# Moving the kernel products of heads 16 to 31 and three of the last eight evacuations in a long-convolution and gated-FFN kernel

## The chip, the cores and the metric

The kernel runs on one core of a Trainium2 chip. The metric is the device time of one execution in microseconds (us), the median of several runs. One execution was also taken by the hardware profiler; its times are those of the profile below.

## The reference

Two parts follow each other. The first is a state-space convolution: each of 64 heads has a kernel of 1024 taps, a sum over 64 complex exponentials, and every sequence (32 of them, masked to its length) is convolved with it. The second is a gated FFN with 4-bit weights, whose result is added to the input.

```python
K = 2.0 * einsum('hn,hnl->hl', Cs, exp(dtA[:, :, None] * arange(L))).real   # 64 heads, 1024 taps
y = irfft(rfft(u_m, n=2 * L) * rfft(K, n=2 * L))[..., :L] + u_m * D[:, None]
y = y * mask
gate, up = y2 @ Wg, y2 @ Wu              # 1024 -> 2752, 4-bit weights, one scale per 128 inputs
out = (gate * sigmoid(gate) * up) @ Wd   # 2752 -> 1024
x = x + out
```

## The kernel before

The kernel K of a head is a product of two small factors, since exp((32a + b) dtA) = exp(32a dtA) exp(b dtA). `tables` and `factors` make the factors on ScalarE (sine, square) and VectorE (lines 189 to 220; `e1t` by L220 is the last of them). `make_kernel` (L397) then forms the product for eight heads on TensorE (L401 for the D term, L403 for the factors, all in f32), ScalarE copies it as f16 (L406), VectorE subtracts the copy for the low f16 half (L407), and two DMAs on SP's queue write both halves to a padded array in DRAM, `kpad` (L409). `toeplitz` (L488, its DMA L499) loads from it, with overlapping rows, a head's Toeplitz matrix of 128 x 2 x 1024 f16 (512 KB).

`conv_head` (L505) convolves one head: 24 matmuls (L521) in 8 steps, and after every second head VectorE multiplies the PSUM result by the mask into `y` (L533), ScalarE rounds it to the f16 tile `xh` (L536), and GpSimd, for the last pair VectorE, makes the low half `xl` (L538). `conv(0)` is heads 0 to 15, `conv(1)` heads 16 to 31. Its PSUM tiles `cq` come from the pool "a", two single banks; the pool "b" holds three pairs of banks. 16 heads are one block of 512 columns of the FFN's input.

The FFN runs as chains. A chain (`gu_one` for one block, `gu_pair` for two, `dn_pair` for the down projection) runs over groups of 128 inputs: four matmuls of 512 columns, then a rescale in place in PSUM by the ratio of two groups' scales, on VectorE or ScalarE, whichever a running estimate, `lag`, has less work for (L584, L587, L604, L608). `gu_one`'s matmuls are L618 (on `xh`) and L619 (on `xl`), `gu_pair`'s L639 and L640, `dn_pair`'s L677, L678 and, for the last group, L680. Up to four chains are under way. `roll` (L706) writes their order by hand, in rounds of one step for each active chain, and advances side generators at set rates: in stage 0, beside the four `gu_one` chains of block 0, `second()` at five steps for each chain step.

The first convolution, ahead of stage 0, is a loop over its 128 steps (L853). At set step numbers it issues other work: step 7 the product of heads 8 to 15, the factors of heads 16 to 31 and two input splits (`kernel_8`), step 40 the product of heads 16 to 23, step 56 the scale ratios, step 72 the product of heads 24 to 31, step 100 the load of the inputs of heads 16 to 19. Every eighth step from 32 to 104 advances the unpacking of the 4-bit weights (loads L552 and L553, VectorE L556 and L566, GpSimd L562). `second()` (L860) then makes the ratios of the down projection, issues the Toeplitz loads of heads 16 to 21, closes the pool `kg`, lets six steps pass and runs `conv(1)`. A scheduler puts the instructions on the engines by priority, so that an instruction can stand somewhat earlier or later in its engine's queue than its place in the source; each engine then works in order.

At the end, `dn_pair` of block 3 adds to the input: ScalarE scales each half of a chain's result into `o` (L693), VectorE adds it to the residual (L694; in the earlier blocks GpSimd does), and SP stores 256 KB (L695).

Of the kernel before, what the change touches and what calls it, by code (L numbers as in the profile page):

```python
# [16 lines left out]
AF = mybir.ActivationFunctionType  # L17
ALU = mybir.AluOpType
# [237 lines left out]
class Core:  # L256
# [410 lines left out]
    def dn_pair(self, k, blk, place):  # L667
        nc = self.nc
        self.need(*(("dn", k, half) for half in range(2)))
        q = self.psum("chq", place)  # L670
        for g in range(GI):
            while blk % 2 == 1 and g < 21 and not self.loaded.get((blk, g)):
                yield
            for j in range(2):
                lw = self.wd[k][:, g, 128 * j:128 * j + 128]
                if g < 21:
                    nc.tensor.matmul(q[:, j], lw, self.ihl[:, g, 0], start=(g == 0), stop=False, skip_group_check=True)  # L677
                    nc.tensor.matmul(q[:, j], lw, self.ihl[:, g, 1], start=False, stop=False, skip_group_check=True)  # L678
                else:
                    nc.tensor.matmul(q[:, j], lw, self.ic[blk % 2], start=False, stop=True, skip_group_check=True)  # L680
            if g < 21:
                self.rescale_two(q, self.rdn[:, 2 * k:2 * k + 2, g:g + 1])
                self.passed[blk, g] = self.passed.get((blk, g), 0) + 1
                if blk % 2 == 0 and self.passed[blk, g] == 4:
                    nc.sync.dma_start(self.ihl[:, g], self.spill[g])
                    self.loaded[blk + 1, g] = True
                yield
        xr = self.res[k] if blk == 3 else self.residual(self.fw, 2 * k, blk)
        o = self.fw.tile([128, 2, 512], F16, name="o", bufs=2)
        self.act(1180)  # L690
        for j in range(2):
            n = 2 * k + j
            nc.scalar.activation(o[:, j], q[:, j], AF.Copy, scale=self.ldn[:, n:n + 1])  # L693
            (nc.gpsimd if blk < 3 else nc.vector).tensor_tensor(xr[:, j], xr[:, j], o[:, j], ALU.add)  # L694
            nc.sync.dma_start(self.io["out"][128 * n:128 * n + 128, 512 * blk:512 * blk + 512], xr[:, j])  # L695
        yield

# [70 lines left out]
def tile_ssm_ffn(ctx, tc, io):  # L768
    nc = tc.nc
    c = Core(ctx, tc, io)  # L770
# [14 lines left out]
    kg = kg_stack.enter_context(tc.tile_pool(name="kg", bufs=1))  # L785
# [49 lines left out]
    def ratios_dn():  # L835
        c.rdn, c.ldn = c.scale_ratios(c.sdn, GH, GI, "dn", [(0, 8, 0, 128, 16.0)])
# [11 lines left out]
    def load_16():  # L848
        c.us[4] = c.conv_load(16)

    events = {7: kernel_8, 40: lambda: c.make_kernel(kg, 16, 8, "b"), 56: ratios_gu,
              72: lambda: c.make_kernel(kg, 24, 8, "b"), 100: load_16}
    for i, _ in enumerate(c.conv(0)):  # L853
        if i in events:
            with c.after("dve" if i == 56 else None):
# [4 lines left out]
    def second():  # L860
        with c.after("dve"):
            ratios_dn()
        for h in range(16, 22):
            c.t0[h] = c.toeplitz(h)
        kg_stack.close()
        wdp = ctx.enter_context(tc.tile_pool(name="wdp", bufs=1))
        c.wd = [wdp.tile([128, GI, 256], F8, name=f"wd{k}") for k in range(4)]
        for _ in range(6):
            yield
        yield from c.conv(1)  # L870

    def slowly(gen, n):
# [65 lines left out]
    def residuals():  # L938
# [4 lines left out]
    convs_it = convs()  # L943
    sides = {
        0: [(unpack_it, RATES["first"][0], False), (second(), RATES["first"][1], True)],
        1: [(unpack_it, RATES["second"], False)],
        2: [(unpack_it, RATES["pairs"], False), (third_it, RATES["third"], False)],
# [82 lines left out]
```

## Time and profile before

| | us |
|---|---|
| median of 3 runs | 1096.97 (1095.69 to 1097.18) |
| profiled execution | 1800.77 |
| its span, first to last instruction | 1798.8 |
| first conv matmul starts | 24.43 |
| last L678 starts | 1787.60 |

The profiled execution had a mean granted TensorE clock of 0.561, and the timed runs are much shorter; a profile's row of TensorE is therefore not that of a timed run. Times in the profile are from the start of the span. PE is TensorE, DVE VectorE, ACT ScalarE, POOL GpSimd; a line such as L533 is a line of the kernel. Brackets at the end of a row give the idle time before it and what ended it. L694 stands eight times on VectorE and 24 times on GpSimd; `chq` is a chain's PSUM tile, `kq` a kernel product's.

### The profile page before, as it was taken

The page shows a single profiled execution, that of the slowest core. Times are in us where ns is not written, and L with a number is a line of the kernel's source. Part 1 is how long each engine was busy: PE and PEld are TensorE (multiplying, and loading weights), DVE is VectorE, ACT ScalarE, POOL GpSimd, SP SyncE. Part 2 cuts the span into 40 slices and gives each one's busy share as a digit, 9 for nine tenths or more (in the row PEclk, how much of TensorE's full clock was granted, in tenths as well). Part 3 has the DMA queues.
Part 4 walks back from the last instruction along what each step waited for, and adds up shares of the span by engine and source line. Part 5 has one row for each costly group of instructions (what it writes and reads, how often), then busy time and mean ns, then how long its engine had stood idle before and what let it go on. Part 6 is the DMA issues. An engine that isn't in the chain of part 4 may idle for free.

```text
span 1094.8 us, 15376 instructions
## 1 busy us (share of the span) xinstructions
PE 1031.6 (94%) x5834; PEld 515.6 (47%) x5834; DVE 786.8 (72%) x903; ACT 777.7 (71%) x1027; POOL 218.0 (20%) x212
## 2 busy tenths in 40 slices
PE   3889989899999999999998999999999999999996
PEld 2667534344444444554556444444444444444443
DVE  8875668888986667874663767766677766776776
ACT  5536768888887677774664677777767777778776
POOL 0342233443431121012003002111111111001100
PEclk9899999999999999998999999999999999999999
DMA  6876223233200203336655001000000000424202
GB/s 203 274 235 197 76 75 122 83 114 100 75 20 20 79 21 97 123 110 211 216 190 203 1 29 68 20 20 20 20 20 20 20 20 15 149 77 132 91 1 77
DMA packets 55169, 99.73 MB, mean 91 GB/s; under 512 B 9396, under 2 KB 10292, under 8 KB 55096
## 3 DMA queue, kind: packets, MB, share of 16 engines
q1 hardware_dynamic: 54520, 98.73, 28.0%
q8 instruction: 45, 0.74, 0.3%
q14 instruction: 28, 0.23, 0.1%
q10 hardware_dynamic: 576, 0.03, 0.0%
HBM read 78.99 MB, written 19.76 MB: 90 GB/s over the span
## 4 chain that ended last, share of the span: by engine, by line
PE 74%; DVE 10%; ACT 5%; DMA 4%; issue 4%; POOL 2%; DVEq 0%; SPq 0%; ACTq 0%; POOLq 0%
PE chq L639 21%; PE chq L640 20%; PE chq L677 11%; PE chq L678 11%; PE cq L521 5%; PE chq L618 2%; PE chq L619 2%; DVE chq L584 2%; ACT chq L608 1%; ACT chq L587 1%; DVE w L566 1%; DVE chq L604 1%; DMA t<-kpad 1%; POOL xr L694 1%; DVE v L652 1%
## 5 line engine op out<-in xcount | busy, mean ns | idle before, releaser
L639 PE MATMUL chq<-xh,w 128*128 128x512 f16 x1216 | 458.1, 379 | 15.6 <-DVE v L652 8.0
L640 PE MATMUL chq<-xl,w 128*128 128x512 f16 x1216 | 456.5, 379 | 0.0
L587 ACT ACTIVATE chq<-chq,gur 128x1024 f32<-128x1024 f32 x312 | 332.3, 1087 | 107.6 <-PE chq L640 106.4
L584 DVE TENSOR_SCALAR chq<-chq,gur 128x1024 f32<-128x1024 f32 x234 | 300.0, 1291 | 118.2 <-PE chq L640 115.6
L608 ACT ACTIVATE chq<-chq,dnr 128x512 f32<-128x512 f32 x336 | 220.7, 661 | 92.7 <-PE chq L678 87.4
L604 DVE TENSOR_TENSOR chq<-chq,dnr 128x1024 f32<-128x1024 f32 x168 | 206.4, 1232 | 96.7 <-PE chq L678 91.8
L677 PE MATMUL chq<-ihl,wd 128*128 128x512 f16 x672 | 255.9, 381 | 6.7 <-DMA ihl<-spill 2.5
L678 PE MATMUL chq<-ihl,wd 128*128 128x512 f16 x672 | 255.7, 381 | 0.0
L640 PEld LDWEIGHTS <-w 128*128 128x128 fp8e4 x1216 | 118.8, 98 | 163.4 <-issue 26.9
L639 PEld LDWEIGHTS <-w 128*128 128x128 fp8e4 x1216 | 118.8, 98 | 147.1 <-POOL spill L303 2.9
L303 POOL TENSOR_TENSOR ihl<-v,ihl 128x512 f16<-128x512 f32 x42 | 48.9, 1164 | 403.9 <-ACT ihl L595 403.9
L521 PEld LDWEIGHTS <-t 128*128 128x128 f16 x1152 | 86.4, 101 | 43.0 <-DMA t<-kpad 5.4
L678 PEld LDWEIGHTS <-wd 128*128 128x128 fp8e4 x672 | 66.0, 98 | 73.2 <-issue 9.5
L677 PEld LDWEIGHTS <-wd 128*128 128x128 fp8e4 x672 | 66.0, 98 | 71.2 <-issue 3.4
L521 PE MATMUL cq<-uh,t 128*128 128x64 f16 (+7 forms) x720 | 93.3, 229 | 6.0 <-DMA t<-kpad 4.7
L538 POOL TENSOR_TENSOR xl<-y,xh 128x512 f16<-128x512 f32 x28 | 36.5, 1305 | 205.0 <-ACT xh L536 169.7
L521 PE MATMUL cq<-ul,t 128*128 128x256 f16 (+3 forms) x360 | 73.8, 229 | 0.1
L652 DVE SCALAR_TENSOR_TENSOR v<-chq,gul,sg 128x1024 f32<-128x1024 f32 x38 | 48.6, 1279 | 15.3 <-PE chq L640 10.4
L608 ACT ACTIVATE chq<-chq,gur 128x512 f32<-128x512 f32 x62 | 40.9, 662 | 20.8 <-PE chq L619 19.8
L618 PE MATMUL chq<-xh,w 128*128 128x512 f16 x128 | 48.8, 385 | 3.4 <-ACT xh L536 2.9
L303 POOL TENSOR_TENSOR spill<-v,spill 128x512 f16<-128x512 f32 x42 | 49.2, 1172 | 9.0 <-ACT spill L595 9.0
L619 PE MATMUL chq<-xl,w 128*128 128x512 f16 x128 | 48.5, 386 | 0.0
(239 smaller groups left out, 717.7 us busy)
## 6 DMA issues: line engine op xcount, KB each, us to landing
t<-kpad SPq DMA_DIRECT2D x48, 512.0 KB, 4.5
spill<-spill SPq DMA_DIRECT2D x42, 256.0 KB, 2.0
ihl<-spill SPq DMA_DIRECT2D x42, 256.0 KB, 2.8
u<-xF SPq DMA_DIRECT2D x12, 512.0 KB, 3.9
xr<-xT SPq DMA_DIRECT2D x12, 512.0 KB, 4.7
out<-xr SPq DMA_DIRECT2D x24, 256.0 KB, 2.5
w<-qgu SPq DMA_DIRECT2D x21, 256.0 KB, 3.9
z<-zc SPq DMA_DIRECT2D x21, 256.0 KB, 3.6
```

The costliest lines, as they stand in the source:

```text
L303: self.nc.gpsimd.tensor_tensor(out, a, b, op)
L521: nc.tensor.matmul(q[:, d:, h % 2, :], t0[:, lw, 128 * d:128 * d + 128], uu[:, 0:8 - d, h % 4, :], start=(d == 0 and k == 0 and h % 2 == 0 ...
L584: self.mark("dve", self.nc.vector.tensor_scalar(q, q, col, None, ALU.mult))
L587: self.mark("act", self.nc.scalar.activation(q, q, AF.Copy, scale=col))
L604: self.mark("dve", self.nc.vector.tensor_tensor(q, q, cols.to_broadcast([128, 2, 512]), ALU.mult))
L608: self.mark("act", self.nc.scalar.activation(q[:, k], q[:, k], AF.Copy, scale=cols[:, k]))
L618: nc.tensor.matmul(q[:, k], lw, xh[:, g, :], start=(g == 0), stop=False, skip_group_check=True)
L619: nc.tensor.matmul(q[:, k], lw, xl[:, g, :], start=False, stop=(g == GH - 1), skip_group_check=True)
L639: nc.tensor.matmul(q[:, b], lw, xh[:, g, :], start=(g == 0), stop=False, skip_group_check=True)
L640: nc.tensor.matmul(q[:, b], lw, xl[:, g, :], start=False, stop=(g == GH - 1), skip_group_check=True)
L677: nc.tensor.matmul(q[:, j], lw, self.ihl[:, g, 0], start=(g == 0), stop=False, skip_group_check=True)
L678: nc.tensor.matmul(q[:, j], lw, self.ihl[:, g, 1], start=False, stop=False, skip_group_check=True)
```

## The change

The product of heads 16 to 23 moves from step 40 to step 95, the end of the twelfth head, and the load of the inputs of heads 16 to 19 from step 100 to 87. The product of heads 24 to 31 leaves the loop; `second()` makes it after twelve of its steps, now in the pool "a", and closes `kg` behind it. In the last block, three of ScalarE's eight scalings go to VectorE, and three of VectorE's eight adds to GpSimd.

```diff
@@ dn_pair
         for j in range(2):
             n = 2 * k + j
-            nc.scalar.activation(o[:, j], q[:, j], AF.Copy, scale=self.ldn[:, n:n + 1])
-            (nc.gpsimd if blk < 3 else nc.vector).tensor_tensor(xr[:, j], xr[:, j], o[:, j], ALU.add)
+            if blk == 3 and j == 1 and k > 0:
+                nc.vector.tensor_scalar(o[:, j], q[:, j], self.ldn[:, n:n + 1], None, ALU.mult)
+            else:
+                nc.scalar.activation(o[:, j], q[:, j], AF.Copy, scale=self.ldn[:, n:n + 1])
+            (nc.gpsimd if blk < 3 or (j == 0 and k < 3) else nc.vector).tensor_tensor(xr[:, j], xr[:, j], o[:, j], ALU.add)
@@ the loop of the first convolution
-    events = {7: kernel_8, 40: lambda: c.make_kernel(kg, 16, 8, "b"), 56: ratios_gu,
-              72: lambda: c.make_kernel(kg, 24, 8, "b"), 100: load_16}
+    events = {7: kernel_8, 56: ratios_gu, 87: load_16, 95: lambda: c.make_kernel(kg, 16, 8, "b")}
@@ second
         for h in range(16, 22):
             c.t0[h] = c.toeplitz(h)
+        for _ in range(12):
+            yield
+        c.make_kernel(kg, 24, 8, "a")
+        yield
         kg_stack.close()
         wdp = ctx.enter_context(tc.tile_pool(name="wdp", bufs=1))
         c.wd = [wdp.tile([128, GI, 256], F8, name=f"wd{k}") for k in range(4)]
-        for _ in range(6):
-            yield
         yield from c.conv(1)
```

## The prediction

> **What bounds it now.** I read the cores' clock and the page first, because everything else depends on them.
>
> ```profile
> span 1798.8 us, 15376 instructions
> ...
> PE 1772.4 (99%) x5834; PEld 701.8 (39%) x5834; DVE 786.1 (44%) x903; ACT 792.9 (44%) x1027; POOL 215.7 (12%) x212
> ...
> PEclk7555555555555555555555555555555555555555
> ```
>
> TensorE is busy 99% of the span, but at a granted clock of 0.561. The profiled execution took 1800.77 us (2 us of it outside the span); the median of the timed runs is 1096.97. At full clock the same TensorE work is 1772.4 x 0.561 = 994 us. So the timed runs had a clock of at least 0.91, and at 1.0 they hold 1097 - 994 = 103 us without TensorE work: 24 before the first convolution, 11 behind the last rescale, 2 outside, and some 66 in waits that this trace hides behind the slow clock. I take 1.0 for the timed runs. So the trace gives the durations of VectorE, ScalarE and the DMAs as they are, TensorE's have to be multiplied by 0.555, and each wait must be set up anew.
>
> Then the timeline around the moved kernel products (columns: start, duration, engine, line, operation):
>
> ```profile
> 44.90 0.41 DVE L220 TENSOR_TENSOR e1t<-e1t,xd 128x256 f32<-128x256 f32 x1
> ...
> 47.65 0.91 PE L403 MATMUL kq<-e2t,e1t 128*32 128x32 f32 x16
> ...
> 48.59 0.37 ACT L406 ACTIVATE kb<-kq 32x256 f16<-32x256 f32 x1 [6.16 <-PE kq L403]
> ...
> 53.43 0.41 DVE L220 TENSOR_TENSOR e1t<-e1t,xd 128x256 f32<-128x256 f32 x1
> ...
> 55.99 0.69 DVE L533 TENSOR_TENSOR y<-cq,mask 128x512 f32<-128x512 f32 x1 [2.16 <-PE cq L521]
> ...
> 72.31 0.69 DVE L533 TENSOR_TENSOR y<-cq,mask 128x512 f32<-128x512 f32 x1 [1.92 <-PE cq L521]
> 73.04 0.62 ACT L536 CAST xh<-y 128x512 f16<-128x512 f32 x1 [4.49 <-DVE y L533]
> ```
>
> The factors of heads 16 to 23 are ready at 45.31 and their product runs at 47.65: no wait at this clock. The last two rows are the hinge: the last copy of the first convolution (heads 14, 15), and its f16 half, without which no chain can start.
>
> Last, the end of the program:
>
> ```profile
> 1790.12 4.16 ACT L693 ACTIVATE o<-chq,dnl 128x512 f16<-128x512 f32 x7
> ...
> 1790.84 1.90 DVE L694 TENSOR_TENSOR xh<-xh,o 128x512 f32<-128x512 f32 x3 [0.47 <-ACT o L693]
> 1792.65 2.49 DVE L694 TENSOR_TENSOR xl<-xl,o 128x512 f32<-128x512 f32 x4
> 1793.36 2.14 SPq L695 DMA_DIRECT2D out<-xl  x4
> ```
>
> ScalarE's evacuations lead, VectorE's adds follow one behind, and the last add ends at 1795.14.
>
> **The change, first part: the products of heads 16 to 31.** Nothing is added: per product two matmuls by L401 and 16 by L403 (0.88 + 0.91 us here, 1.0 at full clock), one copy on ScalarE (0.37), one subtraction on VectorE (0.40) and two DMAs on SP move. In the built order the first goes from the middle of head 7 to behind head 11, the second from the start of head 10 to behind head 15, ahead of the chains.
>
> *Before, at full clock.* One head of the convolution is 11.36 us / 99 matmuls x 24 = 2.75 us, so 1.53. TensorE stands in the middle of head 7 at about 41.0 (29.57, then 6.3 heads, 0.5 for L401, and 1.2 of waiting for the y of heads 0 and 1, which ends at 35.33). It waits there for the factors till 45.31: 4.3 us. Product, rest of head 7, heads 8 and 9: 50.4. The second factors: 53.84 here, but 2.53 us of that was ScalarE held behind the copy of the first product (the 6.16 us wait), so 51.3: another 0.9 us. Then 0.5 for the product and six heads: TensorE ends the convolution at 61.0.
>
> *After.* It waits instead for the Toeplitz loads. Those of heads 8 to 15, issued from 39.65, landed 6.2 us (the first three, median) to 10.1 us behind their issue, head 11's at about 50; a weight load of 256 KB now stands ahead of them in SP's queue, 0.85 us at the some 300 GB/s of the windows from 30 to 50 us. Head 11 runs 50.8 to 52.3, the product takes 1.0, heads 12 to 15 end at 59.4. So TensorE gains 1.6 us of its 5.2, if that counts.
>
> It doesn't, because VectorE is later than both. Take its row at 72.31 and strike the waits that full clock removes: 2.16 + 0.19 + 0.70 + 1.92 on TensorE, and the 2.53: the last y starts at 64.8. TensorE has waited 3.8 us for it. After, one subtraction (0.33 start to start) stands behind that y, and the y of heads 4 and 5 falls into a gap of 0.69 us before 41.65 (0.61 start to start): the last y starts 0.94 earlier, at 63.9. The chains need its f16 half, 1.4 us later: 66.2 before, 65.3 after.
>
> Against that, before used the wait: 17 matmuls of head 16 stand ahead of the first chain matmul, 72.09 to 74.39 here, 2.30 x 0.555 = 1.28 us. After, the second product (1.0) stands there, work that before had hidden in the convolution. So the first part gives -0.94 + 1.28 = **+0.35 us**. The second product's subtraction (0.40) stands ahead of the first rescale; three chains of four matmuls (0.21 each at full clock, 0.85 a chain) cover the 1.23 us rescale only just, so up to 0.4 more. I take 0.35.
>
> SP: the first product's two writes and the loads of heads 16 to 21 now come late. Its subtraction stands behind the y of heads 12 and 13 (61.6 by the strikes above, 60.7 after) and one more step, and ends at 62.3; the write lands 1.9 later, the load 4.7 after that (these slices' rows): 69. Head 16 is first needed at 65.3 + 12 matmuls + a rescale's rest + four matmuls = 68.8. Nil, but with no margin. The second product's writes have a whole half convolution. From about 120 us on TensorE's order is the same again, so nothing further moves.
>
> **Second part: the last evacuations.** Three of ScalarE's seven (0.59 each) go; ScalarE ends at about 1792.6 instead of 1794.3. VectorE loses three adds (GpSimd takes them) and gets three multiplications out of PSUM. The nearest rows:
>
> ```profile
> L584 DVE TENSOR_SCALAR chq<-chq,gur x234: 1282/1293/1295, 205.2 to 1531.5; 128x1024 f32<-128x1024 f32 x117
> ...
> L694 POOL TENSOR_TENSOR xr<-xr,o x24: 1152/1155/1299, 769.2 to 1676.3; 128x512 f32<-128x512 f32 x24
> ...
> L538 POOL TENSOR_TENSOR xl<-y,xh x28: 1153/1157/2582, 36.1 to 934.4; 128x512 f16<-128x512 f32 x28
> ```
>
> A multiplication half as wide is 1.293 less the 0.54 by which L604 (1.233) exceeds L533 (0.692): 0.75 us, 0.69 start to start. [...] In the built order VectorE now does add, mult, mult, add, add, add, mult, add. It still cannot begin before ScalarE's second evacuation, 1790.84: 5 x 0.62 + 3 x 0.69 + 0.1 for the last pair, which depend on each other = 5.3, end 1796.1. Before, 1795.14: **+1.0 us**. VectorE has become the late engine.
>
> The adds on GpSimd start at 1789.7, 1791.4 and 1792.6 and by L694's 1.155 end at 1793.8, ahead of VectorE. [...] If VectorE drew level with ScalarE, this part would give -0.5.
>
> Sum: 0.35 + 1.0 = +1.35 us. On the profiled clock the first part is +0.7 (TensorE would wait for the f16 half where it now has head 16), so 1800.77 becomes 1802.5; at the timed runs' clock 1096.97 becomes 1098.3.
>
> **Rivals.**
> *TensorE's waits count* (faster). If VectorE reaches the last y earlier than I think, the 5.2 us of waits for factors fall out whole, less the tail's 1.0: 1092.8. For it: a wait of 4.3 us on the bounding engine, in-order. Against: VectorE is busy through 30 to 65 and the last y has 3.8 us of slack to give up first. Chance 0.2.
> *The loads of heads 16 to 21 are late* (slower). One mechanism: the subtraction behind the y of heads 12 and 13, the write, then the load, one after another. It decides once the load takes over 4.7 us; the u load of these slices took 7.6. Then head 16 and all of TensorE behind it stand 2.9 us more: 1098.3 + 2.9 = 1101.2. [...] Chance 0.28.
> *It does nothing measurable*: the parts as computed. Chance 0.52, its own range 1095.5 to 1099.5.
>
> **Numbers.** A measurement of this kernel tells about 0.2% (2.2 us) from no change. Faster than 1094.8: the first rival, 0.2. Slower than 1099.2: the second, and the tail's 0.7 with the rescale's 0.4 at once, 0.3. Same 0.5. The range reaches to both rivals: 1092.5 to 1101.5.
>
> **What would show it.** [...] Wrong if the last y moves by several us, if head 16 waits for its load, or if the tail gets shorter.

## The result, and the profile after

The changed kernel takes 1096.42 us (median of 12 runs, 1094.39 to 1098.59), the kernel before, run on the same chip, 1095.03 (12 runs, 1091.93 to 1097.61): 1.0012 of before, 95% interval 0.9998 to 1.0026, so +1.3 us with -0.2 to +2.8. I had predicted +1.35 and, as the likeliest case, that it does nothing measurable. The sum came out; most of its terms, as the experiments show, did not. "Head" is the part of the change at the kernel products, "tail" the part in the last evacuations.

The profile of before fell on a granted clock of 0.561 and cannot be laid beside the one of after, whose clock was 0.987. The first experiment below is therefore the kernel before once more, profiled at 0.986. Its page, and then the page of after (the PEclk row is the granted clock in tenths, by fortieths of the span):

```profile
span 1094.4 us, 15376 instructions
...
PE 1031.0 (94%) x5834; PEld 515.1 (47%) x5834; DVE 786.6 (72%) x903; ACT 777.7 (71%) x1027; POOL 218.2 (20%) x212
...
PEclk9899999999999999998999999999999999999999
```

```profile
span 1096.1 us, 15375 instructions
...
PE 1029.1 (94%) x5834; PEld 515.6 (47%) x5834; DVE 789.6 (72%) x903; ACT 775.9 (71%) x1024; POOL 219.3 (20%) x215
...
PEclk9989999999999999999998999999999999999998
```

TensorE is busy 1031 of 1094 us, not 1772. 63 us of the span are without its work; I had worked out 101, with 994 us of work where busy time times clock is 1031 x 0.986 = 1017 here; why the profile at 0.561 gave less is not settled. The second slice of before and the third of after show what I had not allowed for: an 8 in PEclk, so stretches below full clock inside a run that is otherwise at full clock.

**The head.** TensorE's waits in before (profiled again), then in after. The bracket is the idle time ahead of the row and what ended it:

```profile
45.04 0.69 PE L403 MATMUL kq<-e2t,e1t 128*32 128x32 f32 x16 [3.68 <-DVE e1t L220]
...
64.45 0.27 PE L521 MATMUL cq<-uh,t 128*128 128x256 f16 x1 [1.14 <-DVE y L533]
68.78 0.59 PE L618 MATMUL chq<-xh,w 128*128 128x512 f16 x2 [2.85 <-ACT xh L536]
```

```profile
44.76 6.11 PE L521 MATMUL cq<-ihl,t 128*128 128x256 f16 x72 [3.01 <-DMA t<-kpad]
...
62.09 0.61 PE L401 MATMUL kq<-ihl,cst 1*32 1x256 f32 x2 [0.49 <-DVE y L533]
66.50 1.44 PE L618 MATMUL chq<-xh,w 128*128 128x512 f16 x3 [3.18 <-ACT xh L536]
```

The wait of 3.68 us for factors turned into one of 3.01 us for head 8's Toeplitz load, in the same place. The second product now runs at 62.09, and ahead of the first L618 stands a wait with no matmul of head 16 in it. The last y of the first convolution, on VectorE, in before and in after:

```profile
53.52 0.69 DVE L533 TENSOR_TENSOR y<-cq,mask 128x512 f32<-128x512 f32 x1 [2.52 <-PE cq L521]
...
67.40 0.68 DVE L533 TENSOR_TENSOR y<-cq,mask 128x512 f32<-128x512 f32 x1
```

```profile
65.12 0.68 DVE L533 TENSOR_TENSOR y<-cq,mask 128x512 f32<-128x512 f32 x1
```

It starts 2.28 us earlier, not 0.94, and the first L618 2.28 us earlier too. Yet the last matmul of the second convolution comes later in after. In before, then in after:

```profile
115.19 0.18 PE L521 MATMUL cq<-uh,t 128*128 128x32 f16 x1
```

```profile
117.58 0.18 PE L521 MATMUL cq<-uh,t 128*128 128x32 f16 x1
```

The lead is lost between the two.

**The tail.** ScalarE and VectorE at the end in before, then VectorE, GpSimd and ScalarE in after. (The added line moves L693 to L696 and L694 to L697; L694 is now the multiplication.)

```profile
1084.57 0.68 ACT L693 ACTIVATE o<-chq,dnl 128x512 f16<-128x512 f32 x1
...
1085.71 4.17 ACT L693 ACTIVATE o<-chq,dnl 128x512 f16<-128x512 f32 x7
1086.44 1.90 DVE L694 TENSOR_TENSOR xh<-xh,o 128x512 f32<-128x512 f32 x3 [0.46 <-ACT o L693]
1088.26 2.49 DVE L694 TENSOR_TENSOR xl<-xl,o 128x512 f32<-128x512 f32 x4
```

```profile
1086.62 0.69 DVE L697 TENSOR_TENSOR xh<-xh,o 128x512 f32<-128x512 f32 x1 [2.09 <-ACT o L696]
1087.23 0.75 DVE L694 TENSOR_SCALAR o<-chq,dnl 128x512 f16<-128x512 f32 x1
...
1088.15 0.75 DVE L694 TENSOR_SCALAR o<-chq,dnl 128x512 f16<-128x512 f32 x1 [0.17 <-ACT o L696]
1088.36 1.15 POOL L697 TENSOR_TENSOR xl<-xl,o 128x512 f32<-128x512 f32 x1
1088.82 1.23 DVE L697 TENSOR_TENSOR xh<-xh,o 128x512 f32<-128x512 f32 x1
...
1090.17 0.69 ACT L696 ACTIVATE o<-chq,dnl 128x512 f16<-128x512 f32 x1 [2.05 <-DVE xh L697]
...
1092.28 0.69 DVE L697 TENSOR_TENSOR xl<-xl,o 128x512 f32<-128x512 f32 x1
```

From the start of the last L608 ahead of the scalings to the end of the last add it takes 6.76 us in before (1083.99 to 1090.75) and 8.80 in after (1084.17 to 1092.97): +2.04, not +1.0. Two things lengthen it. VectorE's add at 1088.82, beside GpSimd's third add, takes 1.23 us instead of 0.69, and GpSimd's takes its usual 1.15. And ScalarE waits 2.05 us before its last scaling: `o` has two buffers, and the one it needs is held by an add that now stands behind multiplications. (To the end of the span, the last store included, the tail is 1.5 us longer: from 1083.99 to 1094.4 in before, from 1084.17 to 1096.1 in after.)

### The profile page after: what moved, and what is told of

Read it like the earlier page. It is cut to its first block, busy times and chain, and to the rows that moved or that the text cites. A ratio compares the mean times of both kernels' runs of the same rounds, so it can differ in the third digit from the quotient of the medians.

```text
span 1093.8 us, 15375 instructions
## 1 busy us (share of the span) xinstructions
PE 1027.2 (94%) x5834; PEld 514.6 (47%) x5834; DVE 789.8 (72%) x903; ACT 775.9 (71%) x1024; POOL 219.1 (20%) x215
## 4 chain that ended last, share of the span: by engine, by line
PE 76%; DVE 11%; ACT 5%; issue 4%; DMA 3%; POOL 1%; SPq 0%; DVEq 0%; ACTq 0%; POOLq 0%
PE chq L639 21%; PE chq L640 20%; PE chq L677 12%; PE chq L678 12%; PE cq L521 5%; PE chq L618 2%; PE chq L619 2%; DVE chq L584 2%; ACT chq L608 1%; DMA t<-kpad 1%; DVE chq L604 1%; DVE w L566 1%; ACT chq L587 1%; DVE v L652 1%; DVE ul L484 1%
## 5 line engine op out<-in xcount | busy, mean ns | idle before, releaser
L640 PE MATMUL chq<-xl,w 128*128 128x512 f16 x1216 | 456.0, 379 | 0.0
L608 ACT ACTIVATE chq<-chq,dnr 128x512 f32<-128x512 f32 x336 | 220.7, 661 | 91.5 <-PE chq L678 86.2
L677 PE MATMUL chq<-ihl,wd 128*128 128x512 f16 x672 | 255.1, 380 | 6.9 <-DMA ihl<-spill 2.7
L678 PE MATMUL chq<-ihl,wd 128*128 128x512 f16 x672 | 254.8, 380 | 0.0
L678 PEld LDWEIGHTS <-wd 128*128 128x128 fp8e4 x672 | 65.7, 98 | 72.8 <-issue 8.8
L677 PEld LDWEIGHTS <-wd 128*128 128x128 fp8e4 x672 | 65.8, 98 | 70.9 <-DMA ihl<-spill 2.8
L608 ACT ACTIVATE chq<-chq,gur 128x512 f32<-128x512 f32 x62 | 40.9, 661 | 19.7 <-PE chq L619 18.7
L618 PE MATMUL chq<-xh,w 128*128 128x512 f16 x128 | 48.8, 387 | 4.2 <-ACT xh L536 3.2
L697 POOL TENSOR_TENSOR xr<-xr,o 128x512 f32<-128x512 f32 x24 | 27.7, 1172 | 103.4 <-ACT o L696 101.7
```

The source lines that it names most:

```text
L608: self.mark("act", self.nc.scalar.activation(q[:, k], q[:, k], AF.Copy, scale=cols[:, k]))
L618: nc.tensor.matmul(q[:, k], lw, xh[:, g, :], start=(g == 0), stop=False, skip_group_check=True)
L640: nc.tensor.matmul(q[:, b], lw, xl[:, g, :], start=False, stop=(g == GH - 1), skip_group_check=True)
```

## The experiments

Each ratio is to the kernel before, run on the same chip in the same rounds (medians 1095.0 and 1094.9), with its 95% interval.

**The kernel before, unchanged.**

> The kernel before, unchanged, for a profile at the clock of the timed runs. By my sum: ratio 1.000; TensorE waits some 4.3 us at L403 in the middle of head 7 and under 1 us at head 10; the last y of the first convolution (heads 14, 15) starts at 64.8, 0.3 us earlier than in the changed kernel's profile would mean that this part of the sum had the wrong sign, later means it was right; the first L618 at 66.2 with 17 matmuls of head 16 ahead of it; the last add ends 7.0 us behind the start of the tail on ScalarE. [...]

Ratio 0.9997 (0.9988 to 1.0007). Five kernels with this head (this one and the four that change the tail alone) have the last matmul of the second convolution at 115.19, 115.55, 114.40, 116.40 and 114.61: one profile's milestone is good to about 1 us, and 115.2 is the mean. The last y of the first convolution stands at 66.72 to 68.60 in these five, and at 64.34 to 65.71 in the seven kernels with a changed head, so that lead is larger than the scatter. The half clock at the start of the chains is not the changed kernel's alone: here too the granted clock is 0.50 there, from 69.8 to 73.2.

What moves the milestone is the granted clock. In windows of 1 us of these profiles it is 1.00 or 0.50, and between the two only where a stretch begins or ends; so a window at clock c has (1 - c)/0.5 of its length at half clock, and added up in this way over windows of 1 or 2 us the half-clocked stretches of the profiles are 3.4 us long, or 6.8. In this profile they follow waits of TensorE of 1.8 to 4.3 us, but not every wait brings one (3.83 us with only the first product moved brought none). In pieces of 3.4 us, there are eight ahead of the tail in this profile (from 29, 46, 70, 152, 510 and 596 us on, those at 46 and 510 double), six in after and four from 38 us on in the head part alone (at 45, 66, 510 and 590). The timed runs show the same: over the 67 runs of before that stood beside this one the mean clock of a run goes from 0.984 to 0.992, and each 0.001 less goes with 0.75 us more. A stretch of 3.4 us lowers the mean by 0.0016, so it goes with some 1.2 us (an estimate from these runs). At 150 us, where the stage changes, every kernel waits; here TensorE's wait, and its busy times and clock in that window, in this run and then in after:

```profile
152.21 1.03 PE L639 MATMUL chq<-xh,w 128*128 128x512 f16 x2 [2.54 <-ACT chq L587]
```

```profile
150.00:160.00 10.00, 7.65 (x29) 3.00 (x29) 4.96 (x7) 7.78 (x10) 3.78 (x5) 0.83 0.30 106
```

```profile
154.17 0.83 PE L639 MATMUL chq<-xh,w 128*128 128x512 f16 x2 [2.11 <-ACT chq L587]
```

```profile
150.00:160.00 10.00, 7.73 (x35) 3.22 (x34) 6.18 (x8) 7.82 (x11) 3.67 (x4) 1.00 0.37 131
```

The number behind the POOL entry is the clock: 0.83 of 10 us is 3.4 us at half, 29 matmuls instead of 35, and 1.7 us lost. The profiles of three of the five kernels with the head of before have this stretch (and so has one experiment below); the one with four buffers for `o` waits 2.61 us there and does not have it.

**The tail alone** (the hunk in `dn_pair`; the rest as before).

> Only the evacuations move (three scalings to VectorE, three adds to GpSimd), the kernel products stay. My prediction's second part: +1.0 us. What the changed kernel's profile suggests: ScalarE's last scaling waits 2.05 us for VectorE's add, because the tile o has two buffers, so +1.9 us. The rival that the tail gains: -0.5 us.

1.0020 (1.0010 to 1.0029), +2.2 us. Its end takes 8.80 us (1083.74 to 1092.54), as in after. My +1.0 is below the interval, if only just.

**The head alone** (the other hunks).

> Only the two kernel products (and the load of heads 16 to 19) move, the evacuations stay. My prediction's first part: +0.35 us. If the tail costs 1.9, the whole of +1.4 leaves -0.5 for this part. If TensorE's waits counted whole: -5. If the half clock at the chains' start is the changed kernel's alone: up to +2.3.

0.9994 (0.9985 to 1.0003), -0.7 us, an interval that holds zero and, at its end, my +0.35. With the tail's +2.2 this makes +1.5, near the measured +1.3: the parts add up, and both of my terms were off, in opposite directions. In the profile the last matmul of the second convolution is later than in before, at 116.09; that execution is nevertheless ahead later on (the first L677, where the next stage begins, at 411.11 against 411.81), since it does not have the half clock at 150 us. One profile does not explain a median, but the mean clocks of the runs point the same way: 0.9889 over the 22 runs of this kernel, 0.9872 over the 67 of before, so 0.0017 x 1094 / 0.5 = 3.7 us less at half clock in a run, about one stretch. At 0.75 us for each 0.001 that is worth 1.3 us (an estimate): more than the whole gain, so the rest of the head part costs some 0.6, with the same 0.9 of uncertainty as the -0.7.

**The tail with four buffers for `o`.**

```diff
-        o = self.fw.tile([128, 2, 512], F16, name="o", bufs=2)
+        o = self.fw.tile([128, 2, 512], F16, name="o", bufs=4)
```

> tail_only with four buffers for the tile o instead of two, so that no scaling waits for an earlier add. If that wait makes the difference between +1.0 and +1.9: +1.0 by the bare VectorE chain of eight operations. If the VectorE chain alone is late, as long as tail_only. A gain would say that the chain is not the bound.

1.0011 (1.0000 to 1.0023), +1.2 us; the end takes 8.48 us. ScalarE's scalings now run without a wait, and that takes off 0.3 us in the profile: VectorE's add beside GpSimd's takes 1.51 here instead of 1.24, which gives part of it back. By the profile the buffers are the smaller share; the times (+1.2 against +2.2, with intervals that overlap) do not settle how small.

**Only the three adds go to GpSimd; only the three scalings go to VectorE.**

```diff
+            (nc.gpsimd if blk < 3 or (j == 0 and k < 3) else nc.vector).tensor_tensor(...)
```

```diff
+            if blk == 3 and j == 1 and k > 0:
+                nc.vector.tensor_scalar(o[:, j], q[:, j], self.ldn[:, n:n + 1], None, ALU.mult)
```

> Only three adds of the last block go to GpSimd, ScalarE keeps all eight scalings. My theory: VectorE's multiplications are what lengthens the end; ScalarE's eight scalings still end where they did and the last add follows, so within 0.3 us of before, although an add of VectorE beside a GpSimd add takes 1.2 to 1.5 us instead of 0.69. Rival: the adds side by side are what costs; then about 1 us above before, with VectorE's last add late by that.

> Only three scalings go to VectorE, which keeps all eight adds. VectorE's chain is then eight adds and three multiplications, 8 x 0.62 + 3 x 0.69 + 0.1 = 7.1 us from the second scaling of ScalarE on, against 4.3 us before: 2.8 us above before, no add stretched since GpSimd has none. [...]

The adds alone: 1.0012 (1.0002 to 1.0021), +1.3 us; the end takes 7.54 us (1084.56 to 1092.10), +0.78. My theory had said no change; it fell. VectorE's adds, then GpSimd's:

```profile
1087.02 0.69 DVE L694 TENSOR_TENSOR xh<-xh,o 128x512 f32<-128x512 f32 x1 [2.08 <-ACT o L693]
1088.17 1.17 DVE L694 TENSOR_TENSOR xh<-xh,o 128x512 f32<-128x512 f32 x1 [0.47 <-ACT o L693]
1089.33 2.77 DVE L694 TENSOR_TENSOR xl<-xl,o 128x512 f32<-128x512 f32 x3
```

```profile
1087.64 1.15 POOL L694 TENSOR_TENSOR xh<-xh,o 128x512 f32<-128x512 f32 x1 [0.58 <-ACT o L693]
1088.80 1.55 POOL L694 TENSOR_TENSOR xl<-xl,o 128x512 f32<-128x512 f32 x1
```

VectorE's second add stands beside GpSimd's and takes 1.17 us. The last three take 2.77 together, against 2.49 for four in before. Here GpSimd's third add is stretched as well, to 1.55. VectorE's last add ends 1.37 us behind ScalarE's last scaling (1090.73), in before 0.87, and that scaling itself ends 0.28 later than in before. The rows also show a pattern: VectorE's stretched add ends 0.55 us behind the end of GpSimd's second add (1088.79), and in after, the tail alone and the one with four buffers 0.54 to 0.55 behind the end of the GpSimd add beside it. It looks as if VectorE's add did most of its work only once GpSimd's was over; no run tests this apart.

The scalings alone: 1.0013 (1.0002 to 1.0024), +1.4 us; the end takes 9.12 us (1081.64 to 1090.76), +2.36, where I had said 2.8 and no stretched add. No add is stretched (L697 0.68 to 0.69), and ScalarE waits 1.80 us for `o`. The profile stands near 2.8, but the times' interval (+0.2 to +2.6) leaves 2.8 out. To the end of the span the two profiles are 0.9 (adds) and 1.9 (scalings) longer than before. So either half of the tail part alone makes the end longer: VectorE has too little spare time there, and GpSimd's help costs VectorE most of what it takes off (five adds take 4.63 us, the eight of before 5.08).

**The head part with `conv(1)` at its old step.** In the head part alone 78 matmuls of the second convolution are left when the chains of its stage are issued; in before 57. The 21 are seven steps of three, the 12 + 1 yields ahead of `conv(1)` instead of 6. TensorE's weight loads in after at that place:

```profile
110.38 1.96 PEld L521 LDWEIGHTS <-t 128*128 128x128 f16 x30
112.53 1.59 PEld L521 LDWEIGHTS <-t 128*128 128x128 f16 x24 [0.20 <-DMA t<-kpad]
116.06 1.59 PEld L521 LDWEIGHTS <-t 128*128 128x128 f16 x24 [1.94 <-DMA t<-kpad]
```

Without chain work between, a head takes TensorE 1.6 us; its Toeplitz load, which waits for one of three buffers, lands 5.0 us behind its issue (median of the loads of `t` from 60 to 120 us, in the head part alone; 4.3 in before). TensorE overtakes the loads. The edit, against the head part alone:

```diff
-        for _ in range(12):
+        for _ in range(5):
             yield
         c.make_kernel(kg, 24, 8, "a")
```

> Only the head part, with five steps instead of twelve ahead of the product of heads 24 to 31, so that conv(1) begins at the same step of stage 0 as before. Theory (the late end): in the head part alone conv(1) starts seven steps = 21 matmuls later, so 78 instead of 57 of its matmuls stand alone at the end of stage 0, where TensorE is faster than the Toeplitz loads and waits for them (0.17 and 1.65 us at L521, 111 to 116 us). With five steps these waits are gone, 57 matmuls stand at the end again, and the time is 1.5 to 2.5 us below before (0.998). Rival (the half clock): the lead of 2.3 to 2.7 us at the first L618 is lost to the halved clock at 66 to 70 us; then this is the same as the head part alone, 0.9994 of before.

0.9983 (0.9974 to 0.9991), -1.9 us, 1.2 below the head part alone, though the two intervals still overlap by 0.0006. The clock does not explain it: the mean over the runs is 0.9893 here, 0.9889 in the head part alone. The same 57 matmuls stand at the end without a wait, in one row of the weight loads:

```profile
111.01 3.61 PEld L521 LDWEIGHTS <-t 128*128 128x128 f16 x57
```

**The head part with matmuls that nobody reads** ahead of the chains.

```diff
-            nc.tensor.matmul(c.psum("wq", "b")[:, 0, :128], e1, e2, start=True, stop=True)
+            nc.tensor.matmul(c.psum("wq", "b")[:, 0, :128], e1[:, :128], e2[:, :128], start=True, stop=True)
...
+    busy(24, 16)
     def second():
```

> The head part, and behind the last matmul of the first convolution 16 matmuls that nobody reads (128 columns, f32, some 0.13 us each at full clock, 2.1 us), so that TensorE idles about 2 us instead of 3 to 4 ahead of the first chain. Theory of the half clock: the granted clock of 66 to 71 us is 1.0 instead of 0.5 to 0.7, the matmuls there stand 0.22 instead of 0.43 us apart, and the first 5 us of chains take 1.5 to 2.3 us less; the time is that much below the head part alone if nothing takes it back. Theory of the late end: the loads of the last heads of conv(1) take most of it back, so the wait at L521 between 110 and 118 us grows from 1.8 to over 3 us, and the time is within 0.5 us of the head part alone.

0.9995 (0.9985 to 1.0005), as the head part alone (0.9994). The granted clock is 1.00 from 64 to 75 us, as the theory of the half clock says. (The 16 matmuls are 32 rows and take 4.0 us, not 2.1.) But the product of heads 24 to 31 slid behind the first chain matmuls, where its 1.3 us (from 68.14 and from 69.83) is not hidden: the head part's own half-clocked stretch was 3.4 us long (66.2 to 69.6), 1.7 us of lost work, and 1.7 - 1.3 = 0.4; the waits for late loads are 1.39 us instead of 1.82, another 0.4; the last matmul of the second convolution comes 0.75 earlier (115.34 against 116.09). So the time stays within 0.5 us of the head part alone, but not because the wait at the end grew. The timed runs show a higher clock too: its mean over the 14 runs is 0.9911, against 0.9889. That the time did not fall fits a cost of the moved product; the times do not show it apart from the gain.

**Both products in the middle of the first convolution.**

```diff
-    events = {7: kernel_8, 40: lambda: c.make_kernel(kg, 16, 8, "b"), 56: ratios_gu,
-              72: lambda: c.make_kernel(kg, 24, 8, "b"), 100: load_16}
+    events = {7: kernel_8, 56: ratios_gu, 65: lambda: c.make_kernel(kg, 16, 8, "b"), 87: load_16,
+              112: lambda: c.make_kernel(kg, 24, 8, "b")}
```

> Only the two products move, to steps 65 and 112 of the first convolution, where their factors have long been ready and where head 16's Toeplitz load is still early; everything else as before. TensorE then waits neither for factors nor, at the end, for late loads, and has matmuls of head 16 to do ahead of the first chain. If the halved clock at 66 to 71 us is real lost time, this is 1 to 2 us faster than the head part with five steps (0.9983 of before), so 0.9965 to 0.9975 of before, and the granted clock behind the first L618 is near 1. If it is not, no better than 0.998.

0.9974 (0.9964 to 0.9985), -2.8 us, the fastest of all; the last matmul of the second convolution is at 112.46. Matmuls of head 16 stand ahead of the first L618 again, and TensorE's waits there are 1.50 and 0.96 us. Busy times and granted clock at the start of the chains, in after, then here:

```profile
66.00:68.00 2.00, 1.50 (x4) 0.56 (x4) 1.08 (x2) 0.73 (x2) 0.69 (x2) 0.50 0.76 222
68.00:70.00 2.00, 2.00 (x6) 0.73 (x5) 0.74 (x1) 0.00 (x0) 0.00 (x0) 0.50 1.02 250
70.00:72.00 2.00, 2.00 (x8) 0.68 (x7) 0.89 (x3) 1.32 (x2) 0.00 (x0) 0.62 1.02 369
```

```profile
66.00:68.00 2.00, 1.04 (x13) 0.57 (x11) 1.07 (x2) 0.62 (x1) 0.93 (x2) 1.00 0.40 124
68.00:70.00 2.00, 2.00 (x14) 1.21 (x13) 1.33 (x2) 0.66 (x1) 0.00 (x0) 1.00 0.96 244
70.00:72.00 2.00, 2.00 (x18) 1.29 (x18) 1.90 (x4) 1.61 (x3) 0.00 (x0) 1.00 1.01 302
```

In the same 4 us from 68 on TensorE gets through 14 matmuls in after and 32 here (of mixed widths). This kernel differs from the one with five steps in the matmuls of head 16 too, and the two intervals overlap (0.9964 to 0.9985, 0.9974 to 0.9991). The rows suggest the half clock as the cause of the last 1 us; the timed runs do not bear it out. The mean clock is 0.9883 over the 11 runs of this kernel and 0.9893 over the 22 of the one with five steps: what is won ahead of the chains is not there over a whole run (this profile has a half-clocked stretch at 150 us that the one with five steps does not have). The 17 matmuls of head 16, done in a wait, are the likelier cause; no run takes them alone.

**One product at a time.** In the first kernel that of heads 16 to 23 moves to step 95; in the second that of heads 24 to 31 goes behind the first convolution, with five steps ahead of it.

```diff
+    events = {7: kernel_8, 56: ratios_gu, 72: lambda: c.make_kernel(kg, 24, 8, "b"), 87: load_16,
+              95: lambda: c.make_kernel(kg, 16, 8, "b")}
```

```diff
+    events = {7: kernel_8, 40: lambda: c.make_kernel(kg, 16, 8, "b"), 56: ratios_gu, 87: load_16}
```

> Only the product of heads 16 to 23 moves to step 95, that of heads 24 to 31 stays at step 72. If the 3.7 us wait for the first factors and the halved clock behind it are what made VectorE's y late (2.5 us at 53.5), the last y of the first convolution comes about 2 us earlier here too, as with both moved. No matmul of head 16 stands ahead of the chains (in the built order), so part of it is lost to the halved clock there: 0.998 to 0.9995 of before. If the second product's wait matters as much, the last y gains only half of it and the time is that of before.

> Only the product of heads 24 to 31 moves behind the first convolution (five steps ahead of it), that of heads 16 to 23 stays at step 40. The 3.7 us wait stays, and with it the halved clock behind it: the last y within 0.7 us of before if the first product is what counts, and the time 0.999 to 1.0005 of before. If the second wait counts as much, about 1 us less.

0.9984 (0.9971 to 0.9997) and 0.9982 (0.9973 to 0.9992). The last y starts at 64.67 and at 64.73: each alone brings the whole lead, 2.7 us. (The load of the inputs of heads 16 to 19 is at step 87 in every kernel with a changed head; what it does alone was not run.) The first met its expectation. For the second I had expected 0.7 at most, and 0.999 or more; that fell. TensorE still waits 3.72 us for the first factors there and runs at half clock until about 50.5, but VectorE waits for the y of heads 8 and 9 0.70 us (at 52.27) instead of 2.52. Two things account for it in the rows: in before the L401 of the second product stood in the half-clocked stretch (1.06 us at 46.94), and of TensorE's work behind the wait 5.2 us are at half clock instead of 6.8, 0.8 us of work, together 1.8. Whether the move or the chance of the clock made the stretch end earlier is not settled.

## Why the prediction was right, and where it was not

*The base.* The timed runs at a clock near 1.0: right (0.986). The last y of before at 64.8 was wrong: 67.40. I had struck 2.16 us of VectorE's wait at the y of heads 8 and 9, because TensorE at full clock would be there in time. It was not: behind the wait of 3.68 us for the factors (predicted 4.3) TensorE was granted half clock from 46 to 52.7, and VectorE waited 2.52.

*"if that counts. It doesn't, because VectorE is later than both".* This step failed. TensorE's waits did hold up VectorE, and the last y came 2.28 us earlier, not 0.94. That is the mechanism of my faster rival, which I had given 0.2; the rows do not separate the wait from the half clock that follows it.

*"before used the wait: 17 matmuls of head 16", 1.28 us.* Right: 17 matmuls, 64.45 to 65.8, and they are missing in after.

*"From about 120 us on ... nothing further moves", and that nothing happens up to there.* This step failed. I counted the six and the thirteen yields as order only. They put 21 matmuls more at the end of the second convolution, where the loads set the pace: 2.1 us of waits in after, and 1.2 us in the times between twelve and five steps. The slower rival, late loads, was right in kind and wrong in place: head 16 does not wait, heads 30 and 31 do.

*The half clock ahead of the chains.* The sum has no term for it. After shows it, from 64.7 to 71.5. In these profiles the length of a wait does not decide by itself whether a stretch comes: 2.85 us ahead of the chains is enough in before, and 3.83 us at 45.58 with only the first product moved brought no half clock at all (1.00 from 44 to 58 us). Each such stretch takes 1.7 us of TensorE's work, and some 1.2 us of the time by the estimate above, as much as the terms of my sum, and how many a wait brings differs from profile to profile: near 45 us two in before, one in after.

*Head, the sum.* Predicted +0.35, measured -0.7 (-1.6 to +0.3). In the two profiles up to the last matmul of the second convolution: -2.28 at the first L618; +1.3 for the 17 matmuls; +0.8 for the half clock (5.0 us of work in after, 66.5 to 71.5, 3.4 in before); +0.5 at a weight tile not yet unpacked (TensorE waits 1.23 us for it at 106.58, 0.76 in before at 107.78); +2.1 for the late loads. That makes +2.4, and 117.58 - 115.19 is 2.39; since a milestone is good to about 1 us, and the head part alone stands at 116.09, so close a match is in part chance. The half clock at 150 us, which after's profile does not have, gives 1.7 back, and when the tail starts after is 0.18 behind (1084.17 against 1083.99); the last 0.5 was not traced. So the term that I left out, the half clock, is larger than the +0.35 that I summed. By the mean clocks it is also where the gain of the head part comes from: one stretch less in a run. The 0.6 that this leaves for the rest is near my +0.35, but by errors of 1 to 2 us each that cancel.

*The tail.* Mis-sized: +1.0 against +2.2 (1.1 to 3.2), +2.04 in the profile. The multiplications were right (0.74 to 0.75 us), and so was VectorE as the late engine, 9 us behind the last L678 (1083.75). What failed is "5 x 0.62 + 3 x 0.69 + 0.1 ... = 5.3" from the second scaling on: it takes 6.35 from 1086.62, for VectorE's add beside GpSimd's (0.5), its waits for ScalarE (0.4), and the order of dependent pairs. No run shows the 0.7 that the range holds for the tail: GpSimd's third add takes its median, 1.15 us, in after, in the tail alone and with four buffers (1.55 in the adds alone), and what is longer in all four is VectorE's add beside it or beside the second, 1.17 to 1.51 us instead of 0.69.

The total was right by luck: a head 1.0 better than I said (0.35 + 0.7) met a tail 1.2 worse. Nor does the match prove much, since the measured -0.2 to +2.8 holds anything from no change to twice my sum.

## What to carry to other kernels

When work moves out of a wait, follow the generators and queues behind it to the point where the order is the same again: the steps that a moved call inserts can push the following work to a place where it stands alone and a transfer sets its pace. Do not strike a wait of one engine for another because "at full clock it would be there"; ask first whether the other engine waits, and what it is granted afterwards. An engine that takes over work in a tail must be free there, and the helper must not slow the one it relieves (here VectorE's add took 1.17 to 1.51 us beside GpSimd's, 0.69 alone): take each half of the move by itself before both. Of the places tried in this kernel the best for a product was where its factors are ready and work remains to fill the gap that follows, with the tail left alone: 0.9974 of before.

## What was not expected of the hardware

- Half clock in steps of 3.4 us, 1.7 us of work each, behind waits of TensorE of 1.8 to 4.3 us (in the kernel before, profiled again, TensorE idles 1.8 us between 26 and 30 us and 4.3 between 590 and 600), in a program whose mean clock is 0.99; the wait near 45 us brought two in before (3.68 us), one in after (3.01) and none with only the first product moved (3.83). With sixteen unread matmuls (4.0 us) in the gap ahead of the chains the granted clock was 1.00 from 64 to 75 us. Most of the scatter between runs of one kernel goes with it: 0.75 us for each 0.001 of mean clock (67 runs, correlation -0.84).
- An add of 128x512 f32 on VectorE takes 0.69 us alone and 1.17 to 1.51 beside an add on GpSimd, which itself mostly stays at 1.15 (1.55 once); in all four profiles with both, VectorE's add ends 0.54 to 0.55 us behind the end of GpSimd's.
